# Inverse roots of the last norms by Ln and Exp on ScalarE, and one maximum read straight from PSUM

## The chip, the cores and the metric

The kernel runs on one core of a Trainium2 chip. A core has five engines that run side by side, each taking its own instructions in order: TensorE (in the profile PE, with PEld for its weight loads), VectorE (DVE), ScalarE (ACT), GpSimd (POOL) and SyncE (SP). They work on SBUF; TensorE writes its results to PSUM, which has eight banks of 512 f32 columns per partition. DMA queues move data to and from HBM. The metric is device time in microseconds (us) of one execution.

## The reference, cut to what matters

The inputs are 64 sequences of 64 tokens with 128 features (x) and as many context tokens. Four layers follow one another: layer 0 is relative-position attention with 16 heads of 64; layer 1 is self attention, cross attention and a feed-forward; layer 2 is a gated fusion; layer 3 is a pre-norm transformer block with a mixture of 8 experts, 2 per token. What the change touches lies in layer 3:

```python
def _ln(x, g, b):
    m = x.mean(-1, keepdims=True)
    v = ((x - m) ** 2).mean(-1, keepdims=True)
    return (x - m) / jnp.sqrt(v + EPS) * g + b
...
q = _ln(latents, sa_ln_g, sa_ln_b)
x = latents + _mha(q, q, sa_in_w, sa_in_b, sa_out_w, sa_out_b)
qc = _ln(x, ca_q_ln_g, ca_q_ln_b)
kv = _ln(tokens, ca_kv_ln_g, ca_kv_ln_b)
x = x + _mha(qc, kv, ca_in_w, ca_in_b, ca_out_w, ca_out_b)
return _fuse_moe(x, moe_ln_g, moe_ln_b, router_w, router_b, fc1_w, fc1_b, fc2_w, fc2_b)
```

`_fuse_moe` starts with another `_ln`. `_mha` has 16 heads of 8 and an ordinary softmax: scores, minus their row maximum, exponential, sum.

## The kernel before, in words

The 4096 tokens are cut into 8 groups of 512 (8 sequences each), and x of a group stays in SBUF as a tile of 128 tokens x (4 blocks of 128 features). Layer 0 (`first_layer`) is written out in a fixed order. All the rest is in `other_layers`: each layer part is a Python generator (`self1`, `cross1`, `forward1`, `layer2`, `self3`, `cross3`), which yields between steps. `drive` steps through the running generators round by round: attention parts of successive groups start 4 rounds apart, light ones 2, and the experts' generator (`experts`) fills in between. Outside layer 0 the order on each engine isn't fixed by the text alone: a scheduler that estimates when operands are ready places the instructions, and inserts the waits between engines.

`normalise` (line 263) is the norm without its affine part. For four blocks of 128 features it takes `bn_stats` and `bn_aggr` on DVE (mean and variance into `mv`), adds EPS on DVE, raises to the power -0.5 on POOL (`rs`), multiplies mean and root on DVE (`nmr`), and then writes `(x - mean) * root` with four activations on ACT. It runs 80 times: 16 times in layer 0, 32 times in layers 1 and 2 and 32 times in layer 3. The 32 of layer 3 come through `ln_turned` (line 1230) and through the end of `cross3` (line 1251): per group one before the self attention, two together before the cross attention (context and x, in step through `together`), and one before the router.

`small_heads` (line 922) is the attention of layers 1 and 3. Its `scores` (line 951) fill four PSUM banks per half group, one for each head of a block of four (g = 0 to 3), and then take the tiles in the order 3, 0, 1, 2. With a mask (layer 1) all four are added to the mask on DVE into SBUF. Without one (layer 3) tile 3 is copied to SBUF by ACT, its maximum is taken from that copy by DVE, and POOL subtracts it; tiles 0 to 2 are read from PSUM by DVE for both steps. The other ACT work of the attention is four masked copies of the keys (`km`), one of the queries (`qs`), two of the values (`vb`), and the exponentials of the turned scores (`pT`), eight per group and attention. `layer2` has one Tanh per group, the experts have Gelu, and the router one small Exp (`e2`, shown as e). PSUM tiles come from one pool of seven banks (`pmm`), with an eighth for small results (`extra`).

Of the kernel before, what the change touches and what calls it, by code (L numbers as in the profile page):

```python
# [12 lines left out]
AF = mybir.ActivationFunctionType  # L13
ALU = mybir.AluOpType
AX = mybir.AxisListType

P = 128
B = 64
S = 64
D = 128  # L20
# [13 lines left out]
ROWW = D + 4  # L34
NEG = -1.0e30
EPS = 1e-5
# [58 lines left out]
def kernel(ctx: ExitStack, tc: tile.TileContext, a: dict, out: bass.AP):  # L95
    order = {"on": False}
    nc = Ordered(tc, order)
# [11 lines left out]
    def ctile(shape, name, dtype=F32):  # L109
        return const.tile(shape, dtype, tag=name, name=name)  # L110

    def wtile(shape, tag, bufs, dtype=F32):
        if tag in COMMON:
            return pools["common"].tile(shape, dtype, tag=tag, bufs=COMMON[tag], name=tag)
        return pools["work"].tile(shape, dtype, tag=tag, bufs=bufs, name=tag)

    def pmm(name="mm"):
        return pools["psm"].tile([P, 512], F32, tag="mm", name=name)
# [19 lines left out]
    def v3(ap, n):  # L138
        return ap.rearrange("p (a b) -> p a b", a=n)

    def last(ap, n):

        return ap.unsqueeze(2).to_broadcast([ap.shape[0], ap.shape[1], n])
# [47 lines left out]
    def col(name, i=0):  # L191
        at = _C[name][0] + i
        return cols[:, at : at + 1]
# [8 lines left out]
    make_identity(nc, ident[:, :])  # L202
    nhalf = ctile([P, NBLK], "nhalf")
    nc.gpsimd.memset(nhalf, -0.5)
    xs = [ctile([P, T], f"x{g}") for g in range(NG)]
    bd_small = ctile([P, 6, 8], "bd_small")
    bd = ctile([P, 6, P], "bd")
# [42 lines left out]
    def transpose4(src, width=D):  # L250

        pt = pmm("tr4")
        for k in range(NBLK):
            nc.tensor.transpose(pt[:, k * P : (k + 1) * P], src[:, k * width : k * width + D], ident)
        return pt
# [4 lines left out]
        nc.scalar.copy(t, pt)  # L260
        return t

    def normalise(dst, src, npm=None, width=D):

        st = wtile([P, NBLK, 6], "st6", 4)
        mv = wtile([P, NBLK, 2], "mv", 4)
        rs = wtile([P, NBLK], "rs", 4)
        for k in range(NBLK):
            nc.vector.bn_stats(st[:, k, :], src[:, k * P : (k + 1) * P])
        for k in range(NBLK):  # L270
            nc.vector.bn_aggr(mv[:, k, :], st[:, k, :])
        nc.vector.tensor_scalar(
            rs, mv[:, :, 1:2].rearrange("p a b -> p (a b)"), EPS, None, ALU.add
        )
        nc.gpsimd.tensor_tensor(rs, rs, nhalf, ALU.pow)
        if npm is not None:
            nc.gpsimd.tensor_tensor(rs, rs, npm, ALU.mult)
        yield
        if npm is None:
            nm = wtile([P, NBLK], "nmr", 4)  # L280
            nc.vector.scalar_tensor_tensor(
                nm, mv[:, :, 0:1].rearrange("p a b -> p (a b)"), -1.0, rs, op0=ALU.mult, op1=ALU.mult
            )
        for k in range(NBLK):
            ks = slice(k * P, (k + 1) * P)
            if npm is None:
                nc.scalar.activation(
                    dst[:, k * width : k * width + D], src[:, ks], AF.Identity,
                    scale=rs[:, k : k + 1], bias=nm[:, k : k + 1],
                )  # L290
            else:
                nc.vector.tensor_scalar(
                    dst[:, ks], src[:, ks], mv[:, k, 0:1], rs[:, k : k + 1], ALU.subtract, ALU.mult
                )
# [21 lines left out]
    def add_row(t, r):  # L316
        r = row(r) if isinstance(r, str) else r
        nc.gpsimd.tensor_tensor(v3(t[:, :], NBLK), v3(t[:, :], NBLK), mid(r, NBLK), ALU.add)
# [537 lines left out]
    def other_layers(ends):  # L856
# [44 lines left out]
        def ctx_of(g, phase):  # L901
            key = (g, phase)
            if key not in cts:
                ct = wtile([P, NB, S], "ctx", 3)
                nc.sync.dma_start(
                    ct, a["ctxT"][:, g * T : (g + 1) * T].rearrange("d (b i) -> d b i", i=S)
                )
                cts[key] = ct
            return cts[key]
# [12 lines left out]
        def small_heads(qT, kvT, wq, wk, wv, wo, scale, bias=None, maskb=None, then=None):  # L922
# [8 lines left out]
            for j in range(4):  # L931
# [4 lines left out]
                else:  # L936
                    nc.scalar.activation(
                        km[:, :, j, :], v3(psk[:, :], NB), AF.Identity,
                        scale=m4[:, j : j + 1], bias=bkm[:, bias, j : j + 1],
# [11 lines left out]
            def scores(hb):  # L951
                sc = [pmm("sc") for _ in range(4)]
                for pl in range(2):
                    for b2 in range(2):
                        b = 4 * hb + 2 * pl + b2
                        for g in range(4):
                            rows32 = slice(32 * g, 32 * g + 32)
                            nc.tensor.matmul(
                                sc[g][64 * b2 : 64 * b2 + 64, pl * 256 : (pl + 1) * 256],
                                lhsT=qs[rows32, b * S : (b + 1) * S],  # L960
                                rhs=km[rows32, b, :, :].rearrange("p j k -> p (j k)"),
                                start=True,
                                stop=True,
                            )
                for g in (3, 0, 1, 2):
                    s = wtile([P, 8, S], "s", 10)
                    mx = wtile([P, 8], "mx", 10)
                    s3 = v3(sc[g][:, :], 8)
                    if maskb is not None:
                        nc.vector.tensor_tensor(  # L970
                            s.rearrange("p (r j) k -> p r j k", j=4),
                            sc[g].rearrange("p (r j k) -> p r j k", r=2, j=4),
                            maskb[:, 2 * hb : 2 * hb + 2, :].unsqueeze(2).to_broadcast([P, 2, 4, S]),
                            ALU.add,
                        )
                    elif g == 3:
                        nc.scalar.copy(s, s3)
                    if maskb is not None or g == 3:
                        nc.vector.tensor_reduce(mx, s, axis=AX.X, op=ALU.max)
                        nc.gpsimd.tensor_tensor(s, s, last(mx[:, :], S), ALU.subtract)  # L980
                    else:
                        nc.vector.tensor_reduce(mx, s3, axis=AX.X, op=ALU.max)
                        nc.vector.tensor_tensor(s, s3, last(mx[:, :], S), ALU.subtract)
                    ss[4 * hb + g] = s
# [230 lines left out]
        def together(*gens):  # L1215

            back = [None] * len(gens)
            left = set(range(len(gens)))
            while left:
                for k in sorted(left):  # L1220
                    try:
                        next(gens[k])
                    except StopIteration as end:
                        back[k] = end.value
                        left.discard(k)
                if left:
                    yield
            return back

        def ln_turned(src, g, b, z=None):  # L1230

            z = wtile([P, T], "z", 3) if z is None else z
            yield from normalise(z, src)
            yield
            pt = transpose4(z)
            t = wtile([P, T], "T", 4)
            nc.scalar.activation(t, pt, AF.Identity, scale=col(g), bias=col(b))
            return t
# [12 lines left out]
        def cross3(g):  # L1251
            x = xs[g]
            ct = ctx_of(g, 3)
            pc = transpose4(ct.rearrange("p b i -> p (b i)"))
            cz = wtile([P, T], "z", 4)
            nc.scalar.copy(cz, pc)
            yield
            kvT, qT = yield from together(
                ln_turned(cz, "ckv_g", "ckv_b", cz), ln_turned(x, "cq_g", "cq_b")
            )  # L1260
            add_row(x, obias[:, 1, :])
            yield
            ps = yield from attention(
                qT[:, :], v3(kvT[:, :], NB), in3[:, 1, 0:D], in3[:, 1, D : 2 * D], in3[:, 1, 2 * D :],
                wo3[:, 1, :], sc3, bias=1, then=(lambda: done.update(exponentials=True)) if g == NG - 1 else None,
            )
            nc.vector.tensor_tensor(x, ps, x, ALU.add)
            yield

            zx = wtile([P, NBLK, ROWW], "zx", 4)  # L1270
            yield from normalise(zx.rearrange("p k c -> p (k c)"), x, width=ROWW)
            yield
            pt = transpose4(zx.rearrange("p k c -> p (k c)"), ROWW)
            hT = wtile([P, T], "T", 4)
            nc.scalar.activation(hT, pt, AF.Identity, scale=col("moe_g"), bias=col("moe_b"))
            yield
            yield from router(g, hT, x, zx)
# [223 lines left out]
```

## Time and profile before

| | us |
|---|---|
| median of 3 runs | 1779.1 (1774.51 to 1781.71) |
| the profiled execution | 1766.36 |
| its span in the trace | 1764.6 |

| engine | busy us | share of the span |
|---|---|---|
| PE (matmul) | 1617.1 | 92% |
| DVE | 1214.6 | 69% |
| ACT | 991.9 | 56% |
| POOL | 913.1 | 52% |

Layer 0 lies in the first 750 us or so, layers 1 and 2 from there to about 1240 us, the attention parts of layer 3 from 1070 to 1515 us, and the experts at the end. A line of the page's groups gives an operation as output<-input with its count, its busy time and mean duration, and behind the bar the idle time of its engine just before it and who ended that. Every instruction carries the line of one helper (L74), so groups are told apart by their tiles. The clock column PEclk is the share of full speed that TensorE was granted.

### The profile page before, as it was taken

Reading aid. Unit: us, or ns where it says so; the run is one execution under the profiler, and the core shown is the slowest. Engines: PE = TensorE matmul, PEld = TensorE weight load, DVE = VectorE, ACT = ScalarE, POOL = GpSimd, SP = SyncE. Lnnn points to the kernel's source line nnn. Section 1 sums busy time; section 2 is a strip of 40 time slices with the busy share of each in tenths; the row PEclk is TensorE's granted clock in tenths of the full one; section 3 lists DMA queues with packets and bytes.
Section 4 is the critical chain, followed back from the end, with each engine's and each line's share of the span. In section 5 each row is a group of like instructions: output and inputs, shape, how many; then the busy total and the mean of one; then the engine's idle time right before and its main releaser. Section 6 shows DMA issues by size and latency. Waiting matters only on the chain.

```text
span 1764.6 us, 46242 instructions
## 1 busy us (share of the span) xinstructions
PE 1617.1 (92%) x18026; PEld 1166.4 (66%) x18026; DVE 1214.6 (69%) x3289; ACT 991.9 (56%) x2712; POOL 913.1 (52%) x875
## 2 busy tenths in 40 slices
PE   7799999999999999699998999899888988679995
PEld 4466666666666666477776777667666767557774
DVE  4567686867676767578887786777566874556663
ACT  4365555556464646255665555567677853236663
POOL 2446373737374647467776666444222243554454
PEclk9899999999999999899999998899889987579998
DMA  6756555555545455410010000000000000112143
GB/s 160 159 142 158 127 142 132 136 138 131 139 128 141 132 147 153 138 49 8 11 32 25 23 20 8 13 2 2 8 14 14 2 20 20 55 51 56 54 122 89
DMA packets 215160, 136.78 MB, mean 78 GB/s; under 512 B 38896, under 2 KB 198786, under 8 KB 214816
## 3 DMA queue, kind: packets, MB, share of 16 engines
q1 hardware_dynamic: 186880, 90.54, 21.3%
q10 hardware_dynamic: 23520, 34.75, 6.0%
q0 software_dynamic: 4544, 8.54, 1.4%
q8 instruction: 144, 2.36, 0.6%
q14 instruction: 72, 0.59, 0.1%
HBM read 66.51 MB, written 68.19 MB: 76 GB/s over the span
## 4 chain that ended last, share of the span: by engine, by line
PE 64%; DVE 16%; ACT 7%; POOL 5%; issue 3%; DMA 3%; another core or an unknown queue 0%; SPq 0%; POOLq 0%; ACTq 0%; DVEq 0%
PE av L74 8%; PE psv L74 8%; PE proj L74 7%; PE psk L74 6%; PE pt L74 6%; PE f L74 6%; PE tok L74 5%; PE pbd L74 4%; DVE mx L74 3%; PE psc L74 3%; DVE s L74 3%; PE acc L74 3%; PE sc L74 3%; ACT z L74 3%; PE tr L74 2%
## 5 line engine op out<-in xcount | busy, mean ns | idle before, releaser
L74 ACT ACTIVATE s<-s,nm 128x128 f32<-128x128 f32 x512 | 198.0, 388 | 248.9 <-DVE nm L74 218.7
L74 POOL TENSOR_TENSOR s<-s,sm 128x512 f32<-128x512 f32 x128 | 130.4, 1040 | 256.0 <-DVE sm L74 256.0
L74 PE MATMUL pt<-ident,s 128*128 128x128 f32 x1536 | 213.5, 282 | 24.5 <-ACT kT L74 10.4
L74 POOL TENSOR_TENSOR s<-s,mx 128x512 f32<-128x512 f32 x160 | 164.0, 1045 | 107.1 <-DVE mx L74 106.9
L74 PEld LDWEIGHTS pt<-ident,s 128*128 128x128 f32 x1536 | 176.4, 145 | 45.1 <-issue 15.2
L74 ACT ACTIVATE pT<-pt 128x512 f32<-128x512 f32 x256 | 141.7, 605 | 81.6 <-PE pt L74 76.9
L74 POOL TENSOR_TENSOR rs<-rs,nhalf 128x4 f32<-128x4 f32 x80 | 81.6, 1020 | 191.9 <-DVE rs L74 157.8
L74 POOL TENSOR_TENSOR skew<-skew,mb 128x512 f32<-128x512 f32 x128 | 159.9, 1271 | 37.0 <-DMA skew<-scr 36.5
L74 PEld LDWEIGHTS av<-vb,pT 128*64 128x64 f32 x4096 | 133.7, 144 | 21.2 <-issue 16.5
L74 PE MATMUL av<-vb,pT 128*64 128x18 f32 x4096 | 142.0, 216 | 4.7 <-issue 2.6
L74 DVE TENSOR_REDUCE mx<-s 128x8 f32<-128x512 f32 x160 | 102.9, 675 | 43.8 <-ACT s L74 43.8
L74 POOL DMA_INDIRECT yrows<-km,tob x78 | 76.2, 977 | 100.9 <-DVE m L74 75.3
L74 PE MATMUL psv<-wv,kv 128*128 128x256 f32 x512 | 127.4, 392 | 0.0
L74 PE MATMUL psk<-kv,wk 128*128 128x512 f32 x256 | 127.4, 620 | 0.0
L74 PE MATMUL sc<-km,qs 32*64 32x256 f32 x2048 | 104.7, 420 | 17.2 <-ACT qs L74 12.6
L74 DVE COPY pT<-pt 128x512 f32<-128x512 f32 x128 | 82.2, 683 | 37.5 <-PE pt L74 37.5
L74 PEld LDWEIGHTS psv<-wv,kv 128*128 128x128 f32 x512 | 92.2, 189 | 15.1 <-issue 1.0
L74 PEld LDWEIGHTS av<-pT,v 128*64 128x64 f32 x2048 | 66.6, 138 | 52.8 <-issue 31.1
L74 PEld LDWEIGHTS pbd<-rT,qp 64*128 64x128 f32 x1024 | 63.0, 189 | 58.0 <-DVE qp L74 56.3
L74 DVE TENSOR_TENSOR s<-sc,mb 128x512 f32<-128x512 f32 x128 | 81.9, 680 | 23.1 <-PE sc L74 23.1
L74 DVE TENSOR_TENSOR s<-psc,skew 128x512 f32<-128x512 f32 x128 | 87.5, 683 | 14.7 <-issue 7.3
L74 ACT ACTIVATE z<-z,nmr,rs 128x128 f32<-128x128 f32 x160 | 66.1, 488 | 55.7 <-DVE nmr L74 42.0
(237 smaller groups left out, 3749.0 us busy)
## 6 DMA issues: line engine op xcount, KB each, us to landing
scr<-stage SPq DMA_DIRECT2D x64, 516.0 KB
skew<-scr SPq DMA_DIRECT2D x128, 256.0 KB
hrows<-pad ACTq DMA_DIRECT2D x66, 330.0 KB
ctx<-in_ctxT SPq DMA_DIRECT2D x24, 256.0 KB
km<-hrows SPq DMA_DIRECT2D x78, 66.0 KB
fcw<-in_fc ACTq DMA_DIRECT2D x16, 256.0 KB
kv<-in_xT SPq DMA_DIRECT2D x8, 256.0 KB
kv<-in_ctxT SPq DMA_DIRECT2D x8, 256.0 KB
```

The costliest lines, as they stand in the source:

```text
L74: ins = it(*args, **kw)
```

## The change

`normalise` gets a parameter `root`. With "pow", the default, it is as before. With "ln", which the 32 norms of layer 3 now ask for, the add of EPS on DVE and the power on POOL are left out, and ACT takes the logarithm of variance + EPS (EPS as a bias operand from a new constant tile) and then the exponential of -0.5 times that. In `scores` the maximum of tile 3 without a mask is read from its PSUM bank (`s3`) and not from the SBUF copy (`s`); the copy itself stays, since POOL subtracts from it.

```diff
@@ -202,6 +202,8 @@
     nhalf = ctile([P, NBLK], "nhalf")
     nc.gpsimd.memset(nhalf, -0.5)
+    eps = ctile([P, 1], "eps")
+    nc.gpsimd.memset(eps, EPS)
@@ -260,7 +262,8 @@
-    def normalise(dst, src, npm=None, width=D):
+    def normalise(dst, src, npm=None, width=D, root="pow"):
@@ -269,10 +272,13 @@
-        nc.vector.tensor_scalar(
-            rs, mv[:, :, 1:2].rearrange("p a b -> p (a b)"), EPS, None, ALU.add
-        )
-        nc.gpsimd.tensor_tensor(rs, rs, nhalf, ALU.pow)
+        var = mv[:, :, 1:2].rearrange("p a b -> p (a b)")
+        if root == "pow":
+            nc.vector.tensor_scalar(rs, var, EPS, None, ALU.add)
+            nc.gpsimd.tensor_tensor(rs, rs, nhalf, ALU.pow)
+        else:
+            nc.scalar.activation(rs, var, AF.Ln, bias=eps)
+            nc.scalar.activation(rs, rs, AF.Exp, scale=-0.5)
@@ -976,7 +982,7 @@
                     if maskb is not None or g == 3:
-                        nc.vector.tensor_reduce(mx, s, axis=AX.X, op=ALU.max)
+                        nc.vector.tensor_reduce(mx, s if maskb is not None else s3, axis=AX.X, op=ALU.max)
                         nc.gpsimd.tensor_tensor(s, s, last(mx[:, :], S), ALU.subtract)
@@ -1230,7 +1236,7 @@
-            yield from normalise(z, src)
+            yield from normalise(z, src, root="ln")
@@ -1268,7 +1274,7 @@
-            yield from normalise(zx.rearrange("p k c -> p (k c)"), x, width=ROWW)
+            yield from normalise(zx.rearrange("p k c -> p (k c)"), x, width=ROWW, root="ln")
```

## The prediction

> **What bounds the kernel now.** I read the page first for the span and the engines. PE is busy nearly everywhere, so what counts is whether the change makes PE wait. All 32 changed norms and all 32 changed maxima lie between 1070 and 1520 us. I cut this stretch in three by what the norms in it do and asked for the busy time of the engines in each.
>
> ```profile
> 1070.00:1260.00 190.00, 171.11 (x2045) 124.32 (x2043) 133.05 (x379) 121.24 (x245) 87.51 (x75) 0.91 0.02 6
> 1260.00:1424.00 164.00, 151.06 (x2270) 116.59 (x2268) 114.22 (x395) 127.25 (x247) 44.72 (x42) 0.92 0.03 10
> 1424.00:1520.00 96.00, 82.23 (x859) 65.42 (x855) 55.17 (x267) 35.74 (x70) 45.84 (x46) 0.70 0.08 27
> ```
>
> The columns are stretch, length, then busy time of PE, PEld, DVE, ACT and POOL, the clock, the DMA share and GB/s. The reader is to see the fourth: ACT is busy 64% in the first stage, 78% in the second, 37% in the third; POOL has room everywhere. From POOL's timeline, by its power instructions, 8 changed norms (before self attention) lie in the first, 20 in the second (8 pairs before cross attention, 4 before the router) and 4 in the third.
>
> Next, the groups by shape, for the prices, with ACT's table loads among them:
>
> ```profile
> L74 POOL TENSOR_TENSOR rs<-rs,nhalf 128x4 f32<-128x4 f32 x80 | 81.6, 1020 | 191.9 <-DVE rs L74 157.8 <-DVE cand L74 19.0 <-DVE ci L74 11.0
> L74 DVE TENSOR_SCALAR rs<-mv 128x4 f32<-128x4 f32 x80 | 16.3, 204 | 0.7
> L74 ACT ACTIVATE e<-e 128x4 f32<-128x4 f32 x8 | 1.7, 214 | 14.2 <-DVE e L74 6.9 <-DVE ci L74 4.1 <-DVE cum L74 3.1
> L74 ACT ACT_TABLE_LOAD x2 | 2.6, 1283 | 5.9 <-DMA h<-in_wr 5.9
> L74 DVE TENSOR_REDUCE mx<-s 128x8 f32<-128x512 f32 x160 | 102.9, 675 | 43.8 <-ACT s L74 43.8
> L74 DVE TENSOR_REDUCE mx<-sc 128x8 f32<-128x512 f32 x96 | 62.6, 679 | 0.0
> L74 ACT ACTIVATE qc<-proj,cb 128x512 f32<-128x512 f32 x64 | 44.0, 688 | 19.5 <-DVE qp L74 19.2
> ```
>
> Two table loads serve the whole run: one at the start, after which Exp, Tanh, Relu and copies all run, and one ahead of the first Gelu. ACT's timeline shows how a load sits:
>
> ```profile
> 1540.27 0.46 ACT L74 ACTIVATE vp<-xt,cols 128x128 f32<-128x128 f32 x1 [2.78 <-PE xt L74]
> 1540.74 1.28 ACT L74 ACT_TABLE_LOAD   x1
> 1542.19 1.14 ACT L74 ACTIVATE s<-ht,mb 128x128 f32<-128x128 f32 x4 [0.16 <-PE ht L74]
> ```
>
> It starts as the activation before it ends, and the next one follows 0.17 us behind it, a gap that the profile puts down to PE. So a load costs ACT 1.28 us, at most 1.45. One norm pair of the second stage on ACT:
>
> ```profile
> 1389.38 0.61 ACT L74 COPY oT<-tr 128x512 f32<-128x512 f32 x1
> 1392.88 1.26 ACT L74 ACTIVATE z<-z,nmr,rs 128x128 f32<-128x128 f32 x3 [2.89 <-DVE rs L74]
> 1394.05 0.56 ACT L74 COPY s<-sc 128x512 f32<-128x512 f32 x1
> ```
>
> ACT's only long idle time in a round of about 20 us is the one in which it waits for the norm itself.
>
> **The change part by part.** Removed per norm: the add on DVE (0.20 us x 32 = 6.5 us) and the power on POOL (1.02 x 32 = 32.6 us). Both engines have idle time around them, so their busy time is worth nothing; what they leave is latency of about 0.2 + 1.0 us in front of `nmr`. POOL's queue also loses a blocking wait (107.0 us in 30 waits of `rs` for DVE between 1070 and 1520); behind it stand the bias add to x, the subtraction of tile 3 and, late, the scatters of rows. They may go earlier; PE waits for POOL's subtraction 13.4 us in the whole run, so I take 0 here. No DMA is added or moved on SP or ACT. The new memset of eps is a tenth of a microsecond at the start, before any norm.
>
> Added per norm: a Ln and an Exp of 128x4 on ACT. The small Exp row says 0.21; for Ln's pointer bias I add 0.12, the difference of a 128x128 activation with two pointer operands (0.49, `z`) and one (0.37, Gelu). Together 0.54 us. The larger item is table loads. The trace shows a load wherever the next function isn't served by the set in force, and that this set holds Exp and Tanh together. It can't show which set will be fetched for Ln. Bounds: none of the 32 norms needs more than two loads (into Ln's set and back for the next Exp, which here is the norm's own); at the least, one set serves Ln and Exp and loads come only where Tanh and Ln alternate. I take two: each of the two fetches seen was for the function asked for, not for a pair, and the set in force would then be left for Ln and wanted again at once. So 2 x 1.28 + 0.54 = 3.10 us per norm, 99 us of ACT in all.
>
> The Trainium skill, "ScalarE: Activation LUTs", section "Table sets: the hidden batching unit", speaks for the low end: "ln(x) then exp(x) → 1 TABLE_LOAD", by one set that holds both; the sum would then be the one-set rival's. Its section "What ACT_TABLE_LOAD costs" gives 2.66 us for a switch, drain included; the load at 1540.74 has no such gap behind it, and by that page the sum would grow by 64 x 1.38 = 88 us.
>
> First stage: 8 x 3.10 = 24.8 us on an ACT that has 68.8 us idle. Bounds 0 and 24.8. Here 121 us of ACT work put 35.8 us of ACT on the chain that ended last, 0.30 of it; by the same share +7.
>
> Second stage: 20 x 3.10 = 62.0 us into 36.8 us of idle time. Filled to the last gap, +25; nothing hidden, +62. ACT waits here 13.7 + 4.9 = 18.6 us for the norms themselves (`z` on DVE's rs and nmr), and the first norm of a pair can work in that time. Of the other 18.2 us, waits for PE in the main, I give it 5. So 62.0 - 18.6 - 5 = +38. ACT becomes the bound of this stage. The Ln waits in ACT's queue for DVE's `bn_aggr`, and behind it stand the copy of tile 3, `km`, `qs` and the exponentials `pT`; PE waits for those (scores for qs, products for pT), and DVE for the copy.
>
> Third stage: ACT is idle 60 us, so only latency counts. A load can run before the Ln that waits for its operand, as the one at 1540.74 ran ahead of a waiting Gelu. Then a norm has 0.33 + 1.28 + 0.21 = 1.8 us in place of 0.20 + 1.02 = 1.2, else 3.1: 0.6 to 1.9 more. Four norms give 2 to 8; the chain shows only the last norm's power on it (1.11 us at 1511.96), so I take +2.
>
> The maximum from PSUM: the reduce costs 0.68 either way. What it seems to lift is DVE's wait for ACT's copy (43.8 us in 21 waits). But in layer 0 `qc` on ACT reads only `proj` and its own bias, and still waits 32 times for `qp` on DVE, which reads the same `proj` bank: the first qp runs 0.75 from 11.6, and the idle ACT starts qc at 12.34. So two engines' reads of one bank are put in order here, and the maximum goes on waiting for the copy that stands before it in the program. The bank is then held 0.68 us longer, for 32 tiles. Were the wait lifted, at most the copy on the chain (2.4% of the 164 us, 3.9 us) would be saved; if each of 32 longer holds reached PE, 22 would be lost. PE's waits for a bank freed by DVE are few (2.5, 1.3 and 1.2 us in the first stage), so +1.
>
> Sum: 7 + 38 + 2 + 1 = +48 us. Against the profiled execution's 1766.4 that is 1814; the median of the runs shown is 12.7 us above it, and on that median the forecast is 1827 us.
>
> **Rivals.**
> *One set for Ln and Exp.* ACT then gets 17.3 us of small activations and loads only between Tanh and Ln. By the timeline these alternate 11 times from 1074 to 1237 us: 14.1 us. First stage (14.1 + 4.3) x 0.30 = 5.5, the second 10.8 us in gaps that waited for the power anyway, less some latency saved: +2, or 1781. For it: one such set would do all. Against it: nothing shown asks for a pair.
> *Faster: the power leaves the chain.* POOL's `rs` is 2.4% of the chain from 1060 to 1530, 11.3 us, and the copy of tile 3 another 3.9: 1764. It decides if ACT needs less for a norm than the 1.2 us that DVE and POOL need now, which leaves (1.2 - 0.54) / 1.28, half a load per norm. Against it: the pairs stand among Exps all the time.
> *Dearer switches.* Each load drains ACT for as long again as it takes. 64 x 1.38 = 88 more, 1915. Against it: the 0.17 us seen.
> *The wait moves.* With ACT full, tile 3's copy comes later, DVE waits longer for it and PE is granted less clock as it idles more (0.79 to 0.70 where it starves). This adds to the forecast's case, up to the unhidden 62 of the second stage.
>
> **How the numbers follow.** Chances: two loads per norm 0.83, one set 0.08, faster 0.05, dearer switches 0.04. The likeliest case has its own range: low with stage two filled and the rest at nothing, +25, 1804; high with 62, half of stage one's 24.8, 8 and 4, +86, 1865. It holds nine tenths of its 0.83, 0.75. To leave out no more than 2 in 10 the range goes down through the middle of the one-set case, 1786. About 0.5% (9 us) is what a measurement of this kernel tells from no change: slower takes the first and last case, 0.87; within it the one-set case, 0.08; faster 0.05.
>
> **What would show it.** Right: some 64 more table loads of 1.28 us, between 1070 and 1515 us only; ACT over 90% busy in the stage that was 1260 to 1424, and that stage some 38 us longer; POOL's powers 48 instead of 80; DVE's maximum of tile 3 still released by ACT's copy. Wrong: few loads, or loads in pairs of Lns so that there are far fewer than 64; another order from the scheduler that puts norms where ACT idles; or a gap behind each load.

## The result, and the profile after

The changed kernel takes 1823.99 us (median of 6 runs, 1820.66 to 1831.05) where the kernel before takes 1775.8 (6 runs, 1764.99 to 1781.71): a ratio of the means of 1.0281, 95% interval 1.0244 to 1.0317. That is 48 us more, the size of the forecast's sum. The profiled execution took 1831.05 us with a span of 1829.3; it is the longest of its six, and that of before (1766.36) is shorter than five of the six of before, so the two traces lie 65 us apart where the medians lie 48.

The changed kernel's groups by shape, with the columns of the earlier ones:

```profile
L74 ACT ACT_TABLE_LOAD x64 | 82.1, 1283 | 7.1 <-DMA h<-in_wr 6.0
L74 ACT ACTIVATE rs<-mv,eps 128x4 f32<-128x4 f32 x32 | 9.4, 297 | 13.5 <-DVE mv L74 13.2
L74 ACT ACTIVATE rs<-rs 128x4 f32<-128x4 f32 x32 | 6.5, 204 | 0.3
L74 POOL TENSOR_TENSOR rs<-rs,nhalf 128x4 f32<-128x4 f32 x48 | 49.6, 1034 | 97.3 <-DVE rs L74 92.9
L74 DVE TENSOR_REDUCE mx<-sc 128x8 f32<-128x512 f32 x128 | 81.9, 681 | 45.7 <-ACT s L74 45.2
```

There are 64 table loads where there were 2, each of 1.283 us, and a Ln and an Exp for each of 32 norms at 0.297 and 0.204 us: 1.28 + 1.28 + 0.50 = 3.07 us of ACT for a norm with two loads, forecast 3.10. POOL has 48 powers left of 80, and DVE's maximum still waits for ACT's copy, 45.2 us where it was 43.8. The next lines are the changed kernel's timeline of ACT, over one pair of norms before cross attention:

```profile
1408.48 0.59 ACT L74 COPY oT<-tr 128x512 f32<-128x512 f32 x1 [0.42 <-PE tr L74]
1409.08 1.28 ACT L74 ACT_TABLE_LOAD   x1
1410.38 0.30 ACT L74 ACTIVATE rs<-mv,eps 128x4 f32<-128x4 f32 x1
1410.70 1.28 ACT L74 ACT_TABLE_LOAD   x1
1411.99 0.21 ACT L74 ACTIVATE rs<-rs 128x4 f32<-128x4 f32 x1
1412.21 1.28 ACT L74 ACT_TABLE_LOAD   x1
1413.51 0.30 ACT L74 ACTIVATE rs<-mv,eps 128x4 f32<-128x4 f32 x1
1413.71 0.48 ACT L74 ACTIVATE z<-z,nmr,rs 128x128 f32<-128x128 f32 x1
1414.21 1.28 ACT L74 ACT_TABLE_LOAD   x1
1415.50 0.21 ACT L74 ACTIVATE rs<-rs 128x4 f32<-128x4 f32 x1
```

Where ACT waited 2.89 us for the first norm in the round shown of before, it now works without a gap and fetches a set four times in 6.4 us. Each activation starts 0.01 to 0.02 us behind its load. So the load takes 1.28 us here and no drain beside it. The Trainium skill ("ScalarE: Activation LUTs", "What ACT_TABLE_LOAD costs") gives 1283 ns for the load, which is this row, and about 1380 ns of drain on top, which no row of this trace has.

The stretch that holds the eight pairs and the first router norms, in the changed kernel (columns as in the forecast):

```profile
1285.00:1477.00 192.00, 151.22 (x2084) 116.38 (x2079) 106.90 (x361) 175.04 (x307) 24.47 (x22) 0.86 0.03 8
```

ACT is busy 175.04 of 192 us, 91%, where it was 78%; PE falls from 92% to 79% and its granted clock from 0.92 to 0.86. What PE waits for in the stage of the eight pairs (1290 to 1461 us; us in total, times, longest):

```profile
PE pt L74 <- DVE mx L74: 13.1, 3, 5.0
PE tok L74 <- DVE mx L74: 8.5, 2, 4.6
PE tr L74 <- DVE mx L74: 6.7, 3, 4.5
...
PE sc L74 <- ACT qs L74: 1.8, 1, 1.8
PE pt L74 <- ACT pT L74: 1.8, 1, 1.8
```

Most of it, 28.3 us in the first three lines, is the maximum, which itself waits for ACT's copy of tile 3. By their operands these matmuls don't read the maximum; they wait until the PSUM bank that it reads is free. In the same stage of the kernel before, no wait of PE is over 3.0 us in total. So ACT, nearly full, sets the pace of this stretch, and its late copy is where PE meets it.

By events that all traces have (first normalised x of self attention, first and eighth copy of the turned context, first Gelu, end), in us; the last column is `ln_only` below, which has the same 32 norms and the same number of loads in each part:

| part | before | after | difference | `ln_only` |
|---|---|---|---|---|
| start to the first norm of self attention | 1074.0 | 1078.0 | +4.0 | 1080.4 |
| to the first pair before cross attention | 199.1 | 211.8 | +12.7 | 198.4 |
| to the eighth pair | 135.3 | 171.6 | +36.3 | 175.3 |
| to the first Gelu | 133.8 | 147.0 | +13.2 | 140.5 |
| to the end | 222.4 | 220.8 | -1.6 | 221.7 |

Of these the stretch of the eight pairs is the safest reading. In the traces of four kernels below that leave the router's norms as they were (`max_only`, `max_first`, `ln_self`, `ln_cross`) the part before Gelu takes 138 to 145 us, so its 13.2 is in good part a short reading of before. The first stage is no safer: the eight kernels below whose norms fetch no set in it have 191.5 to 204.0 us. Its rows for before, for the changed kernel and for `ln_only`:

```profile
1074.00:1273.10 199.10, 180.21 (x2175) 131.02 (x2172) 135.90 (x382) 127.03 (x252) 84.56 (x72) 0.91 0.02 7
1078.00:1289.80 211.80, 191.75 (x2163) 140.77 (x2164) 127.61 (x375) 149.52 (x283) 76.33 (x65) 0.86 0.02 5
1080.40:1278.80 198.40, 179.58 (x2163) 130.57 (x2164) 127.10 (x374) 148.55 (x283) 76.34 (x65) 0.92 0.02 5
```

With the same loads and as many matmuls, the changed kernel takes 13.4 us more there than `ln_only`; PE is idle 20.1 and 18.8 us, close to the 18.9 of the kernel before, and nearly all the difference is PE's busy time, at granted clocks of 0.86 and 0.92. Why the clock differs between these executions isn't shown.

### The profile page after: what moved, and what is told of

It is laid out like the page before. It is cut to its first block, busy times and chain, and to the rows that moved or that the text cites. A ratio compares the mean times of both kernels' runs of the same rounds, so it can differ in the third digit from the quotient of the medians.

```text
span 1829.3 us, 46253 instructions
## 1 busy us (share of the span) xinstructions
PE 1644.0 (90%) x18026; PEld 1188.4 (65%) x18026; DVE 1197.8 (65%) x3257; ACT 1087.2 (59%) x2838; POOL 879.8 (48%) x844
## 5 line engine op out<-in xcount | busy, mean ns | idle before, releaser
L74 PE MATMUL pt<-ident,s 128*128 128x128 f32 x1536 | 220.6, 289 | 31.0 <-DVE mx L74 16.2
L74 PEld LDWEIGHTS pt<-ident,s 128*128 128x128 f32 x1536 | 183.7, 149 | 51.2 <-issue 18.2
L74 PEld LDWEIGHTS av<-vb,pT 128*64 128x64 f32 x4096 | 139.4, 147 | 27.0 <-issue 23.3
L74 PE MATMUL av<-vb,pT 128*64 128x18 f32 x4096 | 147.9, 219 | 8.3 <-issue 6.5
L74 DVE TENSOR_REDUCE mx<-sc 128x8 f32<-128x512 f32 x128 | 81.9, 681 | 45.7 <-ACT s L74 45.2
L74 POOL DMA_INDIRECT hrows<-zx,to x64 | 61.9, 967 | 72.8 <-issue 17.3
L74 POOL TENSOR_TENSOR rs<-rs,nhalf 128x4 f32<-128x4 f32 x48 | 49.6, 1034 | 97.3 <-DVE rs L74 92.9
L74 ACT ACTIVATION_READ_ACCUMULATOR s<-s,nm 128x1 f32 x512 | 95.6, 187 | 0.0
```

The costliest lines, as they stand in the source:

```text
L74: ins = it(*args, **kw)
```

## The experiments

Ratios are against the kernel before on the same chip in the same hour; chips differ by some 2%, so microseconds are compared only between kernels that ran together.

**One part alone: the norms** (`ln_only`). The changed kernel with the maximum from SBUF:

```diff
-nc.vector.tensor_reduce(mx, s if maskb is not None else s3, axis=AX.X, op=ALU.max)
+nc.vector.tensor_reduce(mx, s, axis=AX.X, op=ALU.max)
```

> All 32 norms of layer 3 take their root by Ln and Exp, but the maximum of tile 3 is read from the SBUF copy as before. Theory (table loads fill ACT): 64 loads in all and 1816 to 1830 us, a ratio of 1.022 to 1.031, the whole of the change. Rival (the maximum from PSUM holds banks or moves a wait, and is a good part of the loss): 1776 to 1805 us.

Measured: 1820.34 us beside 1773.01, a ratio of 1.0274 (1.0239 to 1.0309), with 64 loads. The norms are the loss, as the theory had it; beside them, the place of the maximum can't be told apart. PE's waits in the stage of the pairs have ACT's copy itself in place of the maximum (`pt`, `tok` and `tr` for `s` on ACT, 21.8 us).

**The other part alone: the maximum** (`max_only`). The kernel before with

```diff
-nc.vector.tensor_reduce(mx, s, axis=AX.X, op=ALU.max)
+nc.vector.tensor_reduce(mx, s if maskb is not None else s3, axis=AX.X, op=ALU.max)
```

> Only the maximum of tile 3 is read from PSUM; all norms keep the power on POOL. Theory (two engines' reads of one bank are put in order): DVE still waits some 44 us for ACT's copy of tile 3, and the ratio is 0.997 to 1.003. Rival (the wait is lifted): the 44 us are gone and 4 to 12 us of time with them, a ratio of 0.993 to 0.998. Rival (banks held longer): up to 22 us more, a ratio of up to 1.012.

Measured: 1.0033 (1.0016 to 1.0051), 5.8 us more. Its waits on DVE, and then on TensorE between 1070 and 1500 us (us in total, times, longest):

```profile
DVE mx L74 <- ACT s L74: 43.8, 21, 7.4
```
```profile
PE pt L74 <- DVE mx L74: 5.7, 4, 2.9
...
PE tok L74 <- DVE mx L74: 2.8, 3, 1.1
```

DVE waits for ACT's copy exactly as long as before, 43.8 us in 21 waits, although the maximum no longer reads the copy. PE now waits for the maximum, 8.5 us in these two lines; in the trace of before the transposes `pt` waited 6.5 us for `s` on DVE in that stretch, and here 2.3. That is what a bank held longer looks like, net some 4 us; that it accounts for all of the 5.8 us is argued, not shown. The time lies at the upper edge of what the theory allowed, and in what the rival of longer held banks allowed; the rival of a lifted wait falls.

**The order turned round** (`max_first`). The maximum from PSUM is written ahead of the copy; norms as before:

```diff
-                    elif g == 3:
-                        nc.scalar.copy(s, s3)
                     if maskb is not None or g == 3:
                         nc.vector.tensor_reduce(mx, s if maskb is not None else s3, axis=AX.X, op=ALU.max)
+                        if maskb is None:
+                            nc.scalar.copy(s, s3)
```

> The maximum from PSUM is written down ahead of ACT's copy of tile 3; all norms keep the power. If reads of one bank by two engines are put in the order of the program, the wait turns round: ACT's copy then waits for DVE's maximum, DVE waits for PE alone, and ACT has the idle time that DVE had (some 20 us). Time: ACT has room in most rounds, so 0.994 to 1.003. If the reads are free of each other, neither waits and the ratio is that of the maximum alone.

Measured: 1.0031 (1.0000 to 1.0061). In its waits:

```profile
ACT s L74 <- DVE mx L74: 29.8, 16, 5.5
```

The wait has changed sides, and DVE's wait for the copy is gone from the list. In these two kernels two reads of one bank are put in the order of the text, whichever engine comes first. It gains no time.

**No switch** (`no_switch`). The changed kernel with Identity in place of Ln. The logarithm is left out:

```diff
-            nc.scalar.activation(rs, var, AF.Ln, bias=eps)
+            nc.scalar.activation(rs, var, AF.Identity, bias=eps)
```

> The changed kernel with Identity in place of Ln, so that the logarithm is left out and the roots are not those of the reference; all waits and engines are the changed kernel's, but Identity needs no table of its own. Theory (table loads): 2 loads in all and 1774 to 1788 us, a ratio of 0.998 to 1.006. Rival (a longer chain of the norm: ACT's queue instead of POOL's, whatever the tables): half of the loss or more stays, 1800 us or above.

Measured: 1765.44 us beside 1773.01, a ratio of 0.9953 (0.9926 to 0.9980), with 2 loads. Against `ln_only` on the same chip that is 54.9 us for 62 loads, 0.89 us each, though `no_switch` has the maximum from PSUM and `ln_only` hasn't. The whole loss goes with the switches; the rival of a longer chain through ACT falls. That the kernel is faster than before was not expected; the next kernels ask whether it's the roots' new place.

**One set, loaded by hand** (`one_set`). Norms before cross attention and the router by Ln and Exp, those before self attention by the power, and behind layer 2's last Tanh one load of a set that serves both (the maximum is read from PSUM, as in the changed kernel):

```diff
+            if g == NG - 1:
+                with tc.issue_after(tanh.ins):
+                    nc.scalar.preload_act_table_set("natural_log_exp_and_others")
```

> The 16 norms before cross attention and the 8 before the router take Ln and Exp, the 8 before self attention keep the power; behind the last Tanh one load of a set that holds both Ln and Exp is placed by hand. The computation is the reference's. Theory (table loads): 3 or 4 loads in all and 1768 to 1785 us, a ratio of 0.995 to 1.005. Rival (ACT's queue is the wrong place for the root of these norms): 1800 us or above. If the loads come all the same (50 of them), the hand-placed set does not stay, and the time is 1810 to 1822.

Measured: 1.0017 (0.9999 to 1.0034), with 3 loads in all:

```profile
L75 ACT ACT_TABLE_LOAD x3 | 3.8, 1283 | 6.4 <-DMA h<-in_wr 6.4
```

24 Lns and 24 Exps without a switch cost nothing that can be measured. So a set that serves both exists, as the Trainium skill says ("ScalarE: Activation LUTs", "Table sets: the hidden batching unit"). Its "1 TABLE_LOAD" for a Ln and an Exp didn't come by itself, with 62 loads more for 32 pairs; here that set is used only where it is put in place by hand.

**Where the norms lie** (`ln_self`, `ln_cross`, `ln_router`). One kind of norm at a time by Ln and Exp, the others by the power, the maximum from PSUM:

```diff
+SELF, CROSS, ROUTER = "ln", "pow", "pow"   # or "pow", "ln", "pow", or "pow", "pow", "ln"
...
-            yield from normalise(z, src, root="ln")
+            yield from normalise(z, src, root=root)
```

> Only the 8 norms before self attention take Ln and Exp; the maximum is read from PSUM as in the changed kernel. The forecast's first stage by itself: 16 to 18 loads, +7 us (bounds 0 and 24.8), so 1778 to 1792, a ratio near 1.004. Rival (the cost goes by the number of norms, a quarter of the loss): +12, a ratio of 1.007.

> Only the 16 norms before cross attention take Ln and Exp; the maximum is read from PSUM. The forecast's second stage without the router's norms: 32 to 34 loads; 16 x 3.1 less the 18.6 us in which ACT waits for these norms, less 5: +26, so 1795 to 1810, a ratio near 1.015. Rival (by the number of norms, half of the loss): +24. Rival (PE bound, ACT's gaps take them): +10 or less.

> Only the 8 norms before the router take Ln and Exp; the maximum is read from PSUM. Four of them lie where ACT is 78% busy and four where it is 37% busy: 4 x 3.1 in the rest of ACT's gaps there and +2 behind, in all +5 to +14, a ratio of 1.003 to 1.008. Rival (by the number of norms): +12.

| norms | loads more | ratio (95%) | less the maximum's 0.0033, of 1776 us |
|---|---|---|---|
| 8, self | 16 | 1.0126 (1.0087 to 1.0164) | 16.5 us, 1.03 per load |
| 16, cross | 28 | 1.0222 (1.0175 to 1.0268) | 33.6 us, 1.20 per load |
| 8, router | 16 | 1.0114 (1.0075 to 1.0153) | 14.4 us, 0.90 per load |

The loads as the trace of the second kernel has them:

```profile
L75 ACT ACT_TABLE_LOAD x30 | 38.5, 1283 | 6.3 <-DMA h<-in_wr 5.8
```

Two of the 16 Lns found the set in place, so 28 and not 32. All three cost more than was expected of them, by the theory and by the rivals, though only the self-attention norms' 16.5 us is beyond the forecast by more than its interval. By the whole time a load costs about one microsecond for each kind of norm, and the intervals (7 to 8 us either way) can't tell the three rates apart. The traces are less even. In `ln_cross` the stage of the pairs takes 159.3 us, 24 more than before with 24 loads in it. In `ln_router` that stage takes 143.4, 8 more with 6 loads, while the part from there to the first Gelu, with 10 more, takes 140.8, within the 138 to 145 of the kernels without them. So the traces don't show that a load costs the same in every stage. The three add up to 64 us, where the whole change without the maximum comes to 0.0248 x 1776 = 44 and `ln_only` to 0.0274 x 1776 = 49; the intervals nearly cover that difference, so whether norms in one program share some of the cost isn't shown.

**Fewer loads** (`paired`). The changed kernel with the two norms before cross attention in one Ln and one Exp:

```diff
-                ln_turned(cz, "ckv_g", "ckv_b", cz), ln_turned(x, "cq_g", "cq_b")
+            kvT, qT = yield from both_turned(cz, x)
...
+            nc.scalar.activation(rs, var, AF.Ln, bias=eps)        # 128x8: both norms
+            nc.scalar.activation(rs, rs, AF.Exp, scale=-0.5)
```

> The changed kernel, with the two norms before cross attention in one Ln and one Exp of 128x8 per group: 16 Lns less, and so some 32 table loads less, at the price that the first norm waits for the second one's statistics. Theory (a load costs 0.94 us of time, 58 us by 62 loads): -26 to -30 us against the changed kernel, 1793 to 1800 beside a kernel before of 1775, a ratio of 1.010 to 1.015. Rival (the longer way of the pair takes it back): 1.018 or above.

Measured: 1.0211 (1.0194 to 1.0229). The expectation counted wrongly: 8 Lns fewer can save 16 loads, not 32, and the trace has 50 in place of 64. The 14 loads go with 1.0281 - 1.0211 = 0.0070, 12 us, give or take 7, or 0.89 per load: the rate of the other runs. The ratio lies in the rival's range; but 14 loads at the theory's own 0.94 give 1.0207, so the run can't tell the two apart.

**Loads that hold ACT only** (`loads_behind`), beside **the 32 norms in one set** (`one_set_32`) and **all 80** (`one_set_80`). In `one_set_32` the set with Ln and Exp is loaded at the start, the maximum is read from the SBUF copy, and the sigmoid that layer 2 makes of a Tanh becomes 1 / (1 + exp(-x)):

```diff
+        nc.scalar.preload_act_table_set("natural_log_exp_and_others")
         nc.sync.dma_start(wq0, a["wq0"])
...
-            nc.scalar.activation(gt, gt, AF.Tanh, scale=0.5)
-            nc.vector.tensor_scalar(gt, gt, 0.5, 0.5, ALU.mult, ALU.add)
+            nc.scalar.activation(gt, gt, AF.Exp, scale=-1.0)
+            nc.vector.tensor_scalar(gt, gt, 1.0, None, ALU.add)
+            nc.vector.reciprocal(gt, gt)
```

`one_set_80` asks for the logarithm in every norm; `loads_behind` is `one_set_32` and, behind each root:

```diff
+            with tc.issue_after(root_done.ins):
+                other = nc.scalar.preload_act_table_set("exp_and_others")
+            with tc.issue_after(other.ins):
+                nc.scalar.preload_act_table_set("natural_log_exp_and_others")
```

> [...] The computation is the reference's. Theory (all of the loss is table switches, and the root on ACT without them is a gain as with Identity in place of Ln, 0.9953): 2 loads, a ratio of 0.988 to 0.998. Rival (the 24 norms with one set, 1.0017, show that the gain with Identity came from elsewhere): 0.999 to 1.004.

> As the kernel with 32 norms in one set, but the 48 norms of layers 0 to 2 take their roots on ACT as well. Theory (the power on POOL is latency of a norm, and POOL's queue waits for it): 0 to 8 us less than with 32, a ratio of 0.984 to 0.997. Rival (those norms lie where PE hides them): the same as with 32, within 3 us.

> The kernel with 32 norms in one set, and behind the Exp of every norm two table loads that nothing needs: 64 loads more, none of them ahead of the norm's own root. Theory (a load costs by the time that it holds ACT): +45 to +65 us over the kernel with 32 norms in one set, as in the changed kernel. Rival (a load costs by the latency that it puts between variance and root): +25 us or less.

| kernel | us | before | ratio (95%) | loads |
|---|---|---|---|---|
| one_set_32 | 1745.28 | 1740.53 | 1.0033 (1.0020 to 1.0046) | 2 |
| one_set_80 | 1731.57 | 1740.53 | 0.9955 (0.9938 to 0.9972) | 2 |
| loads_behind | 1800.67 | 1740.53 | 1.0360 (1.0341 to 1.0379) | 66 |

`loads_behind`'s timeline shows what was added, pairs of loads once the root is there:

```profile
1401.83 0.20 ACT L74 ACTIVATE rs<-rs 128x4 f32<-128x4 f32 x1
1402.04 2.57 ACT L74 ACT_TABLE_LOAD   x2
1404.62 0.60 ACT L74 ACTIVATE pT<-pt 128x512 f32<-128x512 f32 x1
```

64 loads, none of them called for by a norm's own root, cost 1800.67 - 1745.28 = 55.4 us, 0.87 each. That is what the theory expected, and over twice the rival's bound. Not every load is clear of every root: in up to nine of the 32 norms, loads of the norm before run after this one's statistics are there, some 19 us in all. Were all of that felt, 36 of the 55.4 us would be left, so the loss comes in the main from ACT being held. In the traces it lies in the first stage (221.4 us beside 201.5 in `one_set_32`, with 14 loads) and in the stage of the pairs (165.8 beside 138.8, with 34). Over half of these 46.9 us, 27.8, is PE's busy time, at granted clocks of 0.85 and 0.81 beside 0.92 and 0.91; the rest is PE's idle time. From there to the first Gelu, 14 loads more go with 118.9 us beside 117.4. One rival is left: the scheduler places the instructions of each kernel anew. Counting successive matmuls of one kind once, some 110 of 1520 stand elsewhere on PE in `loads_behind` than in `one_set_32`, and some 20 in `no_switch` than in `ln_only`. What the other order is worth isn't shown; two comparisons with unlike orders that give 0.87 and 0.89 speak against its being much.

`one_set_32` is the reference's computation with 2 loads, and the loss is gone there too, but for 0.33%. It didn't gain, against its theory, so nothing shows that the gain of `no_switch` is the roots' place. `one_set_32` pays for something of its own, the reciprocal on DVE:

```profile
L74 DVE RECIPROCAL z<-z 128x512 f32<-128x512 f32 x8 | 26.7, 3342 | 0.1
```

That is 26.7 us more of DVE in layer 2. Whether it hides a gain of the norms, or whether `no_switch` gained from its other roots (its numbers further on are different ones), stays open; no run here separates them. `one_set_80` is 13.7 us faster than `one_set_32`, all of it ahead of layer 3 in the traces (the first norm of self attention at 1064.5 against 1078.0 us), more than the 0 to 8 us expected, and it beats both kernels: 0.45%, some 8 us, under the kernel before, in spite of the reciprocal.

## Why the prediction was right, point by point

**Two loads per norm.** Right: 62 more loads of 1.283 us, a Ln of 0.30 (0.33 worked out from the pointer operands) and an Exp of 0.20 (0.21). There was some luck in it: the ground given, that each of two fetches seen was for the function asked for, couldn't have shown a set that holds a pair. The one-set rival's condition didn't come by itself; put in place by hand for 24 norms, it gave about what the rival said, no change that can be measured (1.0017; the rival's +2 us). The range's low end, 1786, is called the middle of the one-set case, whose own sum is 1781.

**Dearer switches.** Fell: the activations follow their loads within 0.02 us, and a load costs 0.87 to 0.94 us of time by the runs with 62 and 64 loads beside like kernels without them (the 0.94 is (1.0281 - 0.9953) x 1776 / 62), and 48 / 62 = 0.78 beside the kernel before.

**The second stage, +38.** Right in mechanism and near in size: ACT over 90% busy, and the stretch of the eight pairs 36.3 us longer in the traces, 40.0 in `ln_only`. By itself the pair norms cost 33.6 us, 8 either way, where the forecast's method gave +26; in the trace of `ln_cross` that stage is 24 us longer. The wait was named only in part: the forecast had PE wait for `qs` and `pT`, 1.8 us each in the trace after, and the copy of tile 3 hold up DVE alone, where PE waits 28.3 us for that tile's bank. Its rival "the wait moves" had the later copy and the lower clock (0.86 where it was 0.92).

**The first stage, +7.** This is the term that fits least: "by the same share", 0.30 of 24.8 us. Eight norms alone cost 16.5 us, 7 either way, two thirds of what they put on ACT. That share counts the time in which ACT's present work was last, and no run here shows that it carries over to added work. What set the price in its place stays open. The stretch grew by 12.7 us in the changed kernel's trace and by none in that of `ln_only`, with the same loads; PE waited no longer in either, and nearly all the difference between them is busy time of PE, at clocks of 0.86 and 0.92.

**The third stage, +2.** Not told apart: 14.4 us, 7 either way, for all eight router norms alone, which were to come to 5 to 14. In the trace of `ln_router` the excess lies ahead of the eighth pair, not behind it.

**The maximum, +1.** The mechanism was right (the wait stays, and PE waits for the maximum), the size was not: +5.8 us alone (0.16 to 0.51%), where +1 was taken. Beside the norms it doesn't show: 1.0281 with it, 1.0274 without.

**The sum.** 48 against 48 is closer than its terms, and so in part luck. Alone they come to 16.5 + 33.6 + 14.4 + 5.8 = 70, each with 3 to 8 us either way; that in one program they overlap would explain it, and isn't shown. The safe part is the second stage, 36 to 40 of the 48.

**What removal was worth.** Little or nothing for these 32 norms, as taken: with the switches gone, 24 or 32 powers and adds less on POOL and DVE leave the time within 0.5% of before. Two runs hint at more: `no_switch` is 13 us under `max_only` on the same chip, with other roots, and the 48 norms of layers 0 to 2 gave 13.7 us.

## What to carry to other kernels

Before a function is moved to ScalarE, count the table switches against the functions that already run there: here 62 switches of 1.28 us cost 0.8 to 0.9 us of time each, on an engine that was idle four tenths of the time, and the new function itself cost nothing that could be measured. An average hides where that is: most of it came in the stage where ACT was 78% busy. If one set serves both, as for Ln and Exp here, put it in place by hand, and look for the loads in the trace. Reading one PSUM bank from a second engine didn't free that engine of the first here: look for the wait between them before counting on it.

## What was not expected of the hardware

A table load that nothing needs costs as much as one that is asked for: 0.87 us each for 64 in `loads_behind`, 0.89 for 62 in `ln_only`. The loads themselves are exact: 1.283 us for every one in every trace of this case. In `loads_behind` 27.8 of the 46.9 us that two stages lose are not waits of TensorE but matmuls at a lower granted clock, and in the changed kernel TensorE's waits are in the main, 28.3 us, for a PSUM bank that ACT's late copy holds up. And a reciprocal of 128x512 on DVE takes 3.34 us, where the power of 128x4 on POOL takes 1.02 and a logarithm of 128x4 on ACT 0.30.
